# Layer 3's attention front moved under layer 2's third expert, and the targets' factor spread part by part

## The chip, the cores and the metric

One NeuronCore of a Trainium2 chip. The time is the device time of one execution in microseconds (us). Durations of single steps come from one profiled execution. In the profile the engines are PE (TensorE matmul), PEld (TensorE weight load), DVE (VectorE), ACT (ScalarE), POOL (GpSimd) and SP (SyncE, which issues DMAs); a "q" behind a name is that engine's sequencer. L12 is line 12 of the kernel before. Every fp32 matmul appears as two records in the trace, a transpose as one.

## The reference, cut to what matters

A graph of N = 2708 nodes with D = 256 features goes through four layers; each adds a graph step and a feed-forward step to x. What is touched here lies in layers 2 and 3:

```python
# layer 2, attention with one head
wh = h @ W
e = wh @ a[:F_OUT] + (wh @ a[F_OUT:]).T            # target part + source part
e = where(e > 0, e, 0.2 * e); e = where(adj > 0, e, NEG_BIG)
x = x + elu(softmax(e) @ wh)
# layer 2, four experts of 512 hidden units, two per node chosen by scores
for ei in range(4):
    hh = gelu(x @ W1[ei] + b1[ei]); out += g[ei] * (hh @ W2[ei] + b2[ei])
# layer 3, the same attention with four heads of 64 features (no elu), then a
# switch feed-forward of 8 experts with a capacity, one per token
```

Each of these steps reads a layernorm of x.

## The kernel before, in words

**Tiles.** Nodes lie in 22 tiles of 128 rows (the last has 20). Targets are taken in six chunks, five of 512 and one of 148 (CHUNKS). Layer 3's attention uses its own six parts: 256, four times 512, and 404. Loops are unrolled; the only branches in what follows are `tc.If`. Each engine works its instructions in one fixed order; a pool's buffers make an instruction wait until an earlier user of the same buffer is done.

**The attention** (`fast_gat`, L3402) needs no exponential per edge. With f the source part, r the target part and g the largest source part, a weight is adj × max(R[target], Q[source]) once V is scaled by B[source], where R = exp(.8(r + g)) with a bound, Q = exp(−.8(f − g)) and B = exp(f − g) (L3474–L3479). The order is:

1. *Front* (L3425–L3473): GpSimd clears fs and V's column of ones; the weights W and the vectors a are loaded, and VectorE puts W·a beside W (`pr`, L3439, L3445). `features` (L1610) norms x (statistics L1640, L1641, square root on ScalarE L1643, reciprocal L1644, result `fa` on ScalarE L1652 or VectorE L1654), transposes it on TensorE into `ft_ps`, and copies it to `fT` by a helper that alternates VectorE and ScalarE (`copy`, L99 and L101). Each node tile then takes two matmuls into `v_ps` (L3455), a ScalarE copy to V (L3462) and a VectorE copy to fs (L3465).
2. *Extremes* (L2826–L2842), the check of the range (L2849), rel, R, B and Q (to L3479); GpSimd scales V by B, tile by tile (L3482).
3. *Spread* (L141): R is a column per tile. For every chunk and head TensorE transposes it, broadcast over 128 columns, so that each partition holds R of all targets; the result is copied to Rr. All chunks and heads come ahead of the pass: 22 transposes a head, 88 with four heads.
4. *Pass*: for each part, source tile j and head, SyncE loads the adjacency block, VectorE makes the weight tile PT in one instruction (L3525) from Rr, Q and the block, and TensorE accumulates it against V (L3598 with one head, L3673 with four). There are 20 PT buffers (10 with one head). The 20 last source rows go in a short form (Rt, Qt, Vt). The part's end (`finish`, copies at L3557, transposes L3562) and the switch stage's logits and ranks (`after`) are generators of which one step is taken per source tile of the next part.

**Layer 2's experts** (`fast_l2_ffn`). `expert` (L4000) takes for one chunk four hidden blocks of two matmuls each into `h_ps` (2 PSUM buffers), a Gelu on ScalarE into hT (L4013), and then per node tile four matmuls into `y_ps` (L4019). Experts 0 and 1 are computed while the scores are formed, and parked; the parked values are added to x, weighted, by VectorE (L4067). Then expert 2 runs over the six chunks, its results added to x (L4056, L4057). Expert 3 stands behind in a branch on a flag that says whether any node uses it (L4072); with these inputs it is not taken, and the branch skips its body. After the branch comes the setup of the switch stage (`Switch`: constants on GpSimd, L4120 to L4156, weights by SyncE, copies on VectorE at L4262), and then layer 3's attention, in program order; a scheduler may move single instructions among those of other stages on the same engine.

Of the kernel before, what the change touches and what calls it, by code (L numbers as in the profile page):

```python
# [8 lines left out]
F32 = mybir.dt.float32  # L9
# [3 lines left out]
AF = mybir.ActivationFunctionType  # L13
# [5 lines left out]
N = 2708  # L19
D = 256  # L20
# [5 lines left out]
def sz(t):  # L26
    return 128 if t < NT - 1 else TAIL


def blocks(c0, cs):  # L30

    return [((c0 + o) // 128, o, min(128, cs - o)) for o in range(0, cs, 128)]
# [7 lines left out]
def brow(ap, n):  # L40

    return row(ap).to_broadcast([128, n])
# [3359 lines left out]
def fast_gat(k, adjT, W, a, H, elu, col, side, parts=CHUNKS, after=None):  # L3402
# [5 lines left out]

    nc, tc = k.nc, k.tc
    Fo = D // H
    with ExitStack() as ctx:
        keep = ctx.enter_context(tc.tile_pool(name="g", bufs=1))
        V = keep.tile([128, NT, H, Fo + 1], F32, name="V")
        Rr = keep.tile([128, H, N], F32, name="Rr")
        fs = keep.tile([128, 2, H, NT], F32, name="fs")
        R = keep.tile([128, H, NT], F32, name="R")
        Q = keep.tile([128, H, NT], F32, name="Q")
        B = keep.tile([128, H, NT], F32, name="B")  # L3420
        nc.gpsimd.memset(fs, 0.0)
        nc.gpsimd.memset(V[:, :, :, Fo : Fo + 1], 1.0)
        with tc.tile_pool(name="gf", bufs=1) as pf, tc.tile_pool(
            name="gt", bufs=2
        ) as tmp, tc.tile_pool(name="ps_g", bufs=3, space=PSUM) as psv:  # L3425
            fa = pf.tile([128, NT, D], F32, name="fa")
            fT = pf.tile([128, 2, N], F32, name="fT")

            w = pf.tile([128, 2, D + 2 * H], F32, name="w")
            nc.sync.dma_start(w[:, :, :D], W.rearrange("(k p) c -> p k c", p=128))  # L3430
            ar = pf.tile([128, 2, H, Fo], F32, name="ar")
            for s in range(2):
                nc.sync.dma_start(
                    ar[:, s, :, :].rearrange("p h f -> p (h f)"), brow(a[s], D)
                )
            for kk in range(2):
                for s in range(2):
                    pr = tmp.tile([128, H, Fo], F32, name="pr")
                    nc.vector.tensor_tensor(  # L3439
                        pr,  # L3440
                        w[:, kk, :D].rearrange("p (h f) -> p h f", h=H),
                        ar[:, s, :, :],
                        ALU.mult,
                    )
                    nc.vector.tensor_reduce(  # L3445
                        w[:, kk, D + s * H : D + (s + 1) * H], pr, AX.X, ALU.add
                    )
            def project(c0, cs):
                for t, _, p in blocks(c0, cs):
                    value(t, p)  # L3450

            def value(t, p):
                o = psv.tile([128, D + 2 * H], F32, name="v_ps")
                for kk in range(2):
                    nc.tensor.matmul(  # L3455
                        o[:p],
                        lhsT=fT[:, kk, t * 128 : t * 128 + p],
                        rhs=w[:, kk, :],
                        start=(kk == 0),
                        stop=(kk == 1),  # L3460
                    )
                nc.scalar.copy(  # L3462
                    V[:p, t, :, :Fo], o[:p, :D].rearrange("p (h f) -> p h f", h=H)
                )
                nc.vector.tensor_copy(  # L3465
                    fs[:p, :, :, t], o[:p, D:].rearrange("p (s h) -> p s h", s=2)
                )

            k.features(fa, fT, project)
            ex = extremes(k, fs[:, 1, :, :], H, pf, "gx")  # L3470
            spread_check(k, ex, H, col, pf)
            g = ex[:, 0, :, None].to_broadcast([128, H, NT])
            rel = pf.tile([128, H, NT], F32, name="rel")  # L3473
            nc.vector.tensor_tensor(rel, fs[:, 1, :, :], g, ALU.subtract)  # L3474
            nc.vector.tensor_tensor(R, fs[:, 0, :, :], g, ALU.add)
            nc.vector.tensor_scalar(R, R, 0.8, RANGE + 5.0, ALU.mult, ALU.min)
            nc.scalar.activation(R, R, AF.Exp)
            nc.scalar.activation(B, rel, AF.Exp)
            nc.scalar.activation(Q, rel, AF.Exp, scale=-0.8)  # L3479
            for t in range(NT):  # L3480
                p = sz(t)
                nc.gpsimd.tensor_tensor(  # L3482
                    V[:p, t, :, :],
                    V[:p, t, :, :],
                    B[:p, :, t, None].to_broadcast([p, H, Fo + 1]),
                    ALU.mult,
                )
            with tc.tile_pool(name="ps_gs", bufs=2, space=PSUM) as pss:
                for c0, cs in CHUNKS:
                    for h in range(H):  # L3490
                        k.spread(Rr[:, h, c0 : c0 + cs], R[:, h, :], c0, cs, pss)


        every = [h * (H == 4) for h in range(4)]
        last = slice(TAIL), NT - 1
        Vt = k.tail_rows(keep, "Vt", [Fo + 1], F32, [V[last[0], last[1], h, :] for h in every])
        Qt = k.tail_rows(keep, "Qt", [1], F32, [Q[last[0], h, last[1] :] for h in every])
        if H == 1:
            G = len(CHUNKS) - 1
            Rt = keep.tile([128, G + 1, 128], F32, name="Rt")  # L3500
            nc.gpsimd.memset(Rt[:, G, :], 0.0)
            for b in range(4):
                p = slice(32 * b, 32 * b + 32)
                nc.scalar.copy(
                    Rt[p, :G, :],
                    Rr[p, 0, : G * 512].rearrange("p (g b n) -> p b g n", b=4, n=128)[:, b],
                )
            for t, o, n in blocks(*CHUNKS[G]):
                p = slice(o // 4, o // 4 + 32)
                nc.scalar.copy(Rt[p, G, :n], Rr[p, 0, t * 128 : t * 128 + n])  # L3510
# [6 lines left out]
        if H > 1:  # L3517
            pst = ctx.enter_context(tc.tile_pool(name="ps_gt", bufs=2, space=PSUM))
# [3 lines left out]

        def product(PT, R, Q, aj):

            return nc.vector.scalar_tensor_tensor(PT, R, Q, aj, ALU.max, ALU.mult)  # L3525

        made = [None]

        def weights(c0, cs, j, h, aj):

            PT = ptp.tile([128, 512], F32, name="PT")
            made[0] = product(
                PT[:, :cs], Rr[:, h, c0 : c0 + cs], Q[:, h, j : j + 1], aj[:, :cs]
            )
            return PT
# [17 lines left out]
        def finish(c0, cs, i, acc, final):  # L3553
# [4 lines left out]
            yield  # L3558
            for t, o, n in blocks(c0, cs):
# [26 lines left out]

        for i, (c0, cs) in enumerate(parts):
            if H == 1:
# [3 lines left out]
                for j in range(NT - 1):  # L3592
                    PT = weights(c0, cs, j, 0, adjacency(c0, cs, j))
                    for (t, o, n), ac in zip(bl, acc):
                        if n == TAIL:
                            late.append((j, PT[:, o : o + n]))
                            continue
                        nc.tensor.matmul(  # L3598
                            ac[:n],
                            lhsT=PT[:, o : o + n],  # L3600
                            rhs=V[:, j, 0, :],
                            start=(j == 0),
                            stop=False,
                        )
                    if j % 4 == 3 or j == NT - 2:
                        for q, lhsT in late:
                            k.tail_targets(
                                acc[-1], q % 4, q < 4, q > NT - 6, lhsT=lhsT, rhs=V[:, q, 0, :]
                            )
                        late = []  # L3610
# [26 lines left out]
                if c0 + cs == N:  # L3637
                    for _ in side:
                        pass
# [322 lines left out]
def fast_l2_ffn(k, w, edges):  # L3962
# [7 lines left out]
    with ExitStack() as ctx:  # L3970
# [13 lines left out]
        ps1 = ctx.enter_context(tc.tile_pool(name="ps_m1", bufs=2, space=PSUM))  # L3984
# [15 lines left out]
        def expert(e, wt, c0, cs, use):  # L4000
            w1t, w2t = wt
            hT = hp.tile([128, M, 512], F32, name="hT")
            for m in range(M):
# [11 lines left out]
                )  # L4015
            for t, o, n in blocks(c0, cs):
# [9 lines left out]
                use(t, n, y)  # L4026

        with tc.tile_pool(name="el", bufs=1) as pl:
# [33 lines left out]

        for c0, cs in CHUNKS:
# [8 lines left out]
        with tc.If(nc.values_load(flag, min_val=0, max_val=1)):  # L4072
            for c0, cs in CHUNKS:
                expert(E - 1, wts[E - 1], c0, cs, add(E - 1))
# [417 lines left out]
def model(tc, I, out):  # L4492
# [4 lines left out]
    with tc.tile_pool(name="flags", bufs=1) as fp:  # L4497
# [4 lines left out]
        with ExitStack() as ctx:  # L4502
            k = Fast(ctx, tc, I["x"], bad, adjT)
            with tc.tile_pool(name="lists", bufs=1) as lp:
# [35 lines left out]
                fast_gat(k, adjT, I["L2_gnn_W"], I["L2_gnn_a"], 1, True, 2, iter(()))  # L4540
                fast_l2_ffn(k, part(I, "L2_ffn_"), edges)
# [4 lines left out]
            def after(c0, cs, i, psum):  # L4546
# [6 lines left out]
            fast_gat(  # L4553
                k, adjT, I["L3_gnn_W"], I["L3_gnn_a"], 4, False, 3, iter(()), parts, after
            )
# [60 lines left out]
```

## Time and profile before

| | |
|---|---|
| three runs | 2412.81, 2415.03, 2422.92 us; median 2415.03 us |
| the profiled execution | 2413.34 us, of which span 2411.6 us |
| TensorE | busy 2255.9 us, 94% of the span, mean granted clock 0.961 |
| VectorE | busy 1533.7 us, 64% |
| ScalarE | busy 666.4 us, 28% |
| GpSimd | busy 454.6 us, 19% |
| layer 2's expert 2 | TensorE from 1635.2 to 1710.2 us |
| layer 3's front and spread | to the first accumulation at 1776.1 us |
| part 0 of layer 3's pass | to 1808.2 us |
| parts 1 to 5 | to some 2140 us |

A line of the timeline gives the start, the busy time, the engine, the line and operation, output <- inputs, the shapes, how many records are put together (x10), and in brackets the idle time of the engine before it with what ended it. A line of the table of stretches gives start:end and its length, then for each engine the busy time in it (and how many instructions), then the mean granted TensorE clock (1.00 is full), the share of time in which the DMA engines moved data, and GB/s. VectorE also has to do with the part's end in the pass: its 63 us in a part of 512 are 88 weight tiles and some 16 small operations. Some whole-kernel rows:

```profile
L3673 PE MATMUL acc_ps<-PT,V 128*64 128x512 f32 (+4 forms) x2016 | 328.5, 549 | 0.4 <-ACT Rr L101 0.4
L3525 DVE SCALAR_TENSOR_TENSOR PT<-Rr,Q,aj 128x512 f32<-128x512 f32 (+3 forms) x630 | 408.4, 703 | 86.9 <-PE acc_ps L3598 75.1
L4006 PE MATMUL h_ps<-fT,w1t 128*128 128x512 f32 (+1 forms) x288 | 116.4, 554 | 0.3 <-ACT hT L4013 0.2
```

Columns: line, engine, operation, names and shapes, count; then busy us and mean ns of one; then the engine's idle time just before such an instruction, and what ended most of it.

### The profile page before, as it was taken

What the parts mean: (1) busy time and instruction counts of PE and PEld (TensorE: products, weight loads), DVE (VectorE), ACT (ScalarE), POOL (GpSimd) and SP (SyncE); (2) the same over time, 40 slices, a digit from 0 to 9 for tenths busy, and PEclk for the clock granted to TensorE, in tenths of its full rate; (3) what the DMA queues carried; (4) which work ended last, traced back from release to release, by engine and by line L of the source; (5) the groups of instructions that cost most, each with busy time, mean ns of one, the idle gap of its engine ahead of it and who ended that gap; (6) DMA issues with size and microseconds to landing.
All of it is one profiled execution on the core that took longest, in us unless ns stands there. A gap on an engine that the chain in (4) does not pass through costs nothing. (4 is left out here: it accounts for less than half of the span.)

```text
span 2411.6 us, 31812 instructions
## 1 busy us (share of the span) xinstructions
PE 2255.9 (94%) x11620; PEld 1500.7 (62%) x11620; DVE 1533.7 (64%) x3401; ACT 666.4 (28%) x1347; POOL 454.6 (19%) x496
## 2 busy tenths in 40 slices
PE   7999999989899899999799999999889999969997
PEld 4777765577778676777578876666642333325664
DVE  7588888645686558456565562342589999853544
ACT  5433343213655222212230013232321111111121
POOL 1100013004100233565130003420030000002221
PEclk9999999869999999999899998999899999979998
DMA  5244322200756243332245523000033443314430
GB/s 150 66 114 115 113 79 79 73 3 12 239 175 185 67 113 94 83 77 47 69 140 151 144 62 59 21 0 1 10 86 113 114 114 111 92 51 164 128 124 15
DMA packets 158572, 220.00 MB, mean 91 GB/s; under 512 B 30911, under 2 KB 94115, under 8 KB 158404
## 3 DMA queue, kind: packets, MB, share of 16 engines
q1 hardware_dynamic: 126096, 179.84, 25.5%
q0 software_dynamic: 15488, 24.04, 4.8%
q10 hardware_dynamic: 16820, 13.95, 1.8%
q8 instruction: 96, 1.57, 0.3%
q14 instruction: 72, 0.59, 0.1%
HBM read 193.49 MB, written 24.82 MB: 91 GB/s over the span
## 5 line engine op out<-in xcount | busy, mean ns | idle before, releaser
L3525 DVE SCALAR_TENSOR_TENSOR PT<-Rr,Q,aj 128x512 f32<-128x512 f32 (+3 forms) x630 | 408.4, 703 | 86.9 <-PE acc_ps L3598 75.1
L3673 PE MATMUL acc_ps<-PT,V 128*64 128x512 f32 (+4 forms) x2016 | 328.5, 549 | 0.4 <-ACT Rr L101 0.4
L3673 PEld LDWEIGHTS acc_ps<-PT,V 128*64 128x64 f32 (+1 forms) x2016 | 95.2, 122 | 210.2 <-issue 154.6
L1844 PE MATMUL acc_ps<-fa,PT 128*128 128x257 f32 x882 | 215.4, 383 | 1.2 <-DVE out L1864 1.2
L1844 PEld LDWEIGHTS acc_ps<-fa,PT 128*128 128x128 f32 x882 | 163.9, 190 | 66.5 <-issue 33.8
L3598 PE MATMUL acc_ps<-V,PT 128*128 128x257 f32 x882 | 195.4, 382 | 0.8 <-ACT Rr L101 0.6
L3598 PEld LDWEIGHTS acc_ps<-V,PT 128*128 128x128 f32 x882 | 165.8, 190 | 29.8 <-PE acc_ps L3598 2.3
L3304 PE MATMUL h_ps<-xT,w1t 128*128 128x384 f32 x512 | 176.5, 498 | 3.5 <-ACT xT L3295 3.5
L3321 PE MATMUL y_ps<-w2t,hT 128*128 128x256 f32 x768 | 169.8, 380 | 0.0
L2511 PE MATMUL acc_ps<-V,at 128*128 128x257 bf16 x1323 | 156.7, 277 | 10.1 <-DVE at L2502 8.2
L3321 PEld LDWEIGHTS y_ps<-w2t,hT 128*128 128x128 f32 x768 | 144.9, 190 | 21.1
L2511 PEld LDWEIGHTS <-at 128*128 128x128 bf16 x1323 | 128.9, 99 | 32.9 <-DVE at L2502 5.7
L3304 PEld LDWEIGHTS h_ps<-xT,w1t 128*128 128x128 f32 x512 | 95.9, 193 | 68.0 <-ACT xT L3295 8.5
L1816 ACT ACTIVATE PT<-s_ps,rq 128x512 f32<-128x512 f32 (+1 forms) x126 | 79.5, 637 | 174.3 <-PE s_ps L1792 168.7
L3333 POOL DMA_INDIRECT acc<-ys,ids x48 | 92.0, 1916 | 155.1 <-DVE ys L3330 144.7
L1792 PE MATMUL s_ps<-KT,QT 128*128 128x512 f32 (+1 forms) x252 | 116.2, 548 | 2.5 <-ACT PT L1816 1.6
L4019 PE MATMUL y_ps<-w2t,hT 128*128 128x256 f32 (+1 forms) x528 | 117.2, 379 | 0.0
L4006 PE MATMUL h_ps<-fT,w1t 128*128 128x512 f32 (+1 forms) x288 | 116.4, 554 | 0.3 <-ACT hT L4013 0.2
L3003 POOL DMA_INDIRECT xe<-fd,idg x48 | 79.7, 1661 | 194.7 <-DVE early_f L3034 180.3
L1817 DVE SCALAR_TENSOR_TENSOR PT<-aj,PT 128x512 f32<-128x512 int32 (+1 forms) x126 | 79.2, 633 | 57.9 <-ACT PT L1816 57.5
L4442 PE MATMUL y_ps<-w2t,hT 128*128 128x256 f32 (+1 forms) x512 | 112.8, 379 | 0.0
L4019 PEld LDWEIGHTS y_ps<-w2t,hT 128*128 128x128 f32 (+1 forms) x528 | 97.7, 186 | 22.3 <-issue 8.2
(743 smaller groups left out, 3353.0 us busy)
## 6 DMA issues: line engine op xcount, KB each, us to landing
aj<-in_adjT SPq DMA_DIRECT2D x399, 256.0 KB, 2.7
w1t<-in_L_ffn_W SPq DMA_DIRECT2D x8, 1024.0 KB
w2t<-in_L_ffn_W SPq DMA_DIRECT2D x8, 1024.0 KB
w1t<-in_L_ffn_w SPq DMA_DIRECT2D x8, 1024.0 KB, 5.6
w2t<-in_L_ffn_w SPq DMA_DIRECT2D x8, 1024.0 KB
aj<-in_adjT SPq DMA_DIRECT2D x63, 74.0 KB, 1.9
fd<-fa ACTq DMA_DIRECT2D x9, 512.0 KB, 3.2
aj<-in_adjT SPq DMA_DIRECT2D x21, 202.0 KB, 2.5
```

The lines of the kernel that those rows point to most:

```text
L1792: nc.tensor.matmul(s[:, :cs], lhsT=QT[:, j * 128 : j * 128 + 128], rhs=KT[:, c0 : c0 + cs], start=True, stop=True,)
L1844: nc.tensor.matmul(ac, lhsT=PT[:, o : o + n], rhs=fa[:, j, :], start=j == 0, stop=False)
L2511: nc.tensor.matmul(ac[:, c:], lhsT=at[:, o : o + n], rhs=V[:, j, r], start=j == 0 and q == 0, stop=False, skip_group_check=True,)
L3304: nc.tensor.matmul(hp, lhsT=w1t[:, kk, m * 128 : (m + 1) * 128], rhs=self.xT[:, kk, :], start=(kk == 0), stop=(kk == 1),)
L3321: nc.tensor.matmul(y, lhsT=self.hT[:, m, i * 128 : (i + 1) * 128], rhs=w2t[:, m, :], start=(m == 0), stop=(m == M - 1),)
L3333: add = nc.gpsimd.indirect_dma_start(out=acc, out_offset=bass.IndirectOffsetOnAxis(ap=self.ids[:, i : i + 1], axis=0), in_=ys, in_offset=None,
L3525: return nc.vector.scalar_tensor_tensor(PT, R, Q, aj, ALU.max, ALU.mult)
L3598: nc.tensor.matmul(ac[:n], lhsT=PT[:, o : o + n], rhs=V[:, j, 0, :], start=(j == 0), stop=False,)
L3673: nc.tensor.matmul(w.pop("out"), **w)
L4006: nc.tensor.matmul(o[:, :cs], lhsT=w1t[:, kk, m * 128 : (m + 1) * 128], rhs=fT[:, kk, c0 : c0 + cs], start=(kk == 0), stop=(kk == 1),)
L4019: nc.tensor.matmul(y[:n], lhsT=hT[:, m, o : o + n], rhs=w2t[:, m, :], start=(m == 0), stop=(m == M - 1),)
L4442: nc.tensor.matmul(y[:n], lhsT=hT[:, m, o : o + n], rhs=w2t[:, m, :], start=(m == 0), stop=(m == M - 1),)
```

## The change

**Front as an object.** The front and the factors become a class `GatFront`. `all` runs it at once as before (layer 2's attention, where the transposes and value products are asked for chunk by chunk as before; as scheduled, the transposes of all chunks are over sooner, ahead of more of the products). `chunk` is a generator that does one chunk of nodes in steps: norm, the two groups of transposes with their copy, and the value products tile by tile. `ready` forms the extremes and the factors, now R ahead of rel, and the check of the range after them; GpSimd's scaling of V ends it.

**Under the third expert.** In `fast_l2_ffn` the branch with expert 3 stands ahead of expert 2's chunks, and the loading of layer 3's W and a, the two memsets and the products with a (`then()`) are asked for just behind it. When expert 2 is through with a chunk, that chunk's front becomes `side[0]`, of which one step is taken after each hidden block and each node tile of the next chunk; what is left is done before the next. `h_ps` gets a third buffer, and a pool of three `v_ps` buffers stands beside it. Layer 3's tiles come from the other end of the on-chip memory, so that they wait for nothing of layer 2. As scheduled, the loads and the products then stand in the last stage of layer 1 on SyncE and VectorE, ahead of the reload of x, and the memsets of layer 2's front ahead of the last scatter on GpSimd. The setup of the switch stage comes behind `ready`.

**Spread by parts.** The pass begins after spread(0); spread(1) is taken in steps, one head a source tile, within part 0, and spread(i + 2) in part i + 1, between the two halves of part i's end. All its copies are on ScalarE, and it uses the `o_ps` buffers of the part's end. With one head the short form Rt of R is filled part by part too.

The diff, cut:

```diff
+class GatFront:
+    def __init__(self, k, W, a, H, pool, tmp):
...
+    def chunk(self, c0, cs, pool, psum):
+        k, bl = self.k, blocks(c0, cs)
+        t0 = bl[0][0]
+        fa = pool.tile([128, 4, D], F32, name="fa")
+        fT = pool.tile([128, 2, 512], F32, name="fT")
+        yield from k.norm_chunk(pool, fa, t0, len(bl))
+        for kk in range(2):
+            p = psum()
+            for t, o, m in bl:
+                k.nc.tensor.transpose(
+                    p[:, o : o + m],
+                    fa[:m, t - t0, kk * 128 : (kk + 1) * 128],
+                    k.ident[:m, :m],
+                )
+            k.copy(fT[:, kk, :cs], p[:, :cs])
+            yield
+        for t, o, m in bl:
+            self.value(t, m, lambda kk: fT[:, kk, o : o + m], psum)
+            yield
+
+    def ready(self, col):
...
+        ex = extremes(k, fs[:, 1, :, :], H, self.tmp, "gx")
+        g = ex[:, 0, :, None].to_broadcast([128, H, NT])
+        rel = self.tmp.tile([128, H, NT], F32, name="rel")
+        nc.vector.tensor_tensor(R, fs[:, 0, :, :], g, ALU.add)
+        nc.vector.tensor_scalar(R, R, 0.8, RANGE + 5.0, ALU.mult, ALU.min)
+        nc.scalar.activation(R, R, AF.Exp)
+        nc.vector.tensor_tensor(rel, fs[:, 1, :, :], g, ALU.subtract)
+        nc.scalar.activation(B, rel, AF.Exp)
+        nc.scalar.activation(Q, rel, AF.Exp, scale=-0.8)
+        spread_check(k, ex, H, col, self.tmp)
+        for t in range(NT):
+            p = sz(t)
+            vt = self.V[:p, t, :, :]
+            nc.gpsimd.tensor_tensor(
+                vt, vt, B[:p, :, t, None].to_broadcast([p, H, D // H + 1]), ALU.mult
+            )
...
-            with tc.tile_pool(name="ps_gs", bufs=2, space=PSUM) as pss:
-                for c0, cs in CHUNKS:
-                    for h in range(H):
-                        k.spread(Rr[:, h, c0 : c0 + cs], R[:, h, :], c0, cs, pss)
...
-        if H > 1:
-            pst = ctx.enter_context(tc.tile_pool(name="ps_gt", bufs=2, space=PSUM))
+        pst = ctx.enter_context(tc.tile_pool(name="ps_gt", bufs=2, space=PSUM))
...
+        def spread(i):
+            if i >= len(parts):
+                return
+            c0, cs = parts[i]
+            for h in range(H):
+                p = psum()
+                for t, o, n in blocks(c0, cs):
+                    nc.tensor.transpose(
+                        p[:, o : o + n],
+                        R[:n, h, t : t + 1].to_broadcast([n, 128]),
+                        k.ident[:n, :n],
+                    )
+                nc.scalar.copy(Rr[:, h, c0 : c0 + cs], p[:, :cs])
+                yield
+            if H == 1:
+                for t, o, n in blocks(c0, cs):
+                    p = slice(o // 4, o // 4 + 32)
+                    nc.scalar.copy(Rt[p, i, :n], Rr[p, 0, t * 128 : t * 128 + n])
+                yield
...
             for o_, ac in zip(oT, acc):
                 nc.scalar.copy(o_[:, :cs], ac[:, :cs])
             yield
+            yield from spread(i + 2)
...
+        for _ in spread(0):
+            pass
+        side = spread(1)
         for i, (c0, cs) in enumerate(parts):
...
                     PT = weights(c0, cs, j, 0, adjacency(c0, cs, j))
+                    next(side, None)
...
-                if c0 + cs == N:
-                    for _ in side:
-                        pass
+                side = spread(i + 2)
                 continue
...
-def fast_l2_ffn(k, w, edges):
+def fast_l2_ffn(k, w, edges, then):
...
-        ps1 = ctx.enter_context(tc.tile_pool(name="ps_m1", bufs=2, space=PSUM))
+        ps1 = ctx.enter_context(tc.tile_pool(name="ps_m1", bufs=3, space=PSUM))
...
                 nc.scalar.activation(
                     hT[:, m, :cs], o[:, :cs], AF.Gelu, bias=b1[:, e, m : m + 1]
                 )
+                next(side[0], None)
...
                 use(t, n, y)
+                next(side[0], None)
...
+        with tc.If(nc.values_load(flag, min_val=0, max_val=1)):
+            for c0, cs in CHUNKS:
+                expert(E - 1, wts[E - 1], c0, cs, add(E - 1))
+        steps = then()
         for c0, cs in CHUNKS:
...
             for e in range(EARLY, E - 1):
                 expert(e, wts[e], c0, cs, add(e))
-        with tc.If(nc.values_load(flag, min_val=0, max_val=1)):
-            for c0, cs in CHUNKS:
-                expert(E - 1, wts[E - 1], c0, cs, add(E - 1))
+            for _ in side[0]:
+                pass
+            side[0] = steps(c0, cs)
+        for _ in side[0]:
+            pass
...
+                right = dict(side="right")
+                keep = c3.enter_context(tc.tile_pool(name="g3", bufs=1, **right))
...
+                    two = c4.enter_context(tc.tile_pool(name="g3c", bufs=2, **right))
+                    ps = c4.enter_context(
+                        tc.tile_pool(name="ps_g3", bufs=3, space=PSUM, **right)
+                    )
...
+                    return lambda c0, cs: made[0].chunk(c0, cs, two, psum)
...
+            front = made[0]
+            front.ready(3)
+            c4.close()
```

## Prediction

> **What bounds the kernel now.** I read the mean clock and span first, then the table of stretches around the places that the diff touches, then the timeline inside the stretch in which TensorE idles, and last the chain of waits, to see that this stretch is on it. All times are us of one profiled execution.
>
> ```profile
> core 0: us, PE busy (x) PEld busy (x) DVE busy (x) ACT busy (x) POOL busy (x), PEclk, DMA share, GB/s
> ...
> 1709.00:1722.00 13.00, 1.40 (x7) 0.59 (x6) 9.07 (x39) 2.21 (x5) 3.20 (x17) 0.70 0.17 45
> 1722.00:1751.00 29.00, 28.82 (x132) 22.65 (x131) 16.27 (x74) 16.23 (x41) 0.00 (x0) 0.90 0.00 1
> 1751.00:1776.00 25.00, 16.57 (x91) 12.30 (x91) 20.36 (x45) 8.78 (x17) 18.71 (x30) 0.86 0.24 65
> 1776.00:1808.20 32.20, 32.12 (x354) 16.43 (x354) 29.94 (x72) 2.46 (x7) 0.00 (x0) 1.00 0.40 108
> 1808.20:1872.20 64.00, 64.00 (x372) 18.20 (x372) 63.61 (x103) 8.67 (x21) 1.71 (x2) 1.00 0.40 112
> 1872.20:1938.30 66.10, 66.10 (x390) 20.17 (x390) 62.80 (x105) 10.24 (x29) 4.20 (x4) 1.00 0.41 116
> ```
>
> The rows are: the end of layer 2's third expert to the first transpose of layer 3's front; that front (transposes, then the value products); the extremes and the spread of the factor R; part 0 of the pass (256 targets); parts 1 and 2 (512 each). TensorE is idle or cold only in the first three; in parts 1 and 2 both it and VectorE have almost no slack. The timeline says what each edge of the idle stretch waits for:
>
> ```profile
> 1721.84 2.37 PE L1610 MATMUL ft_ps<-ident,fa 128*128 128x128 f32 x10 [11.60 <-DVE fa L1654]
> ...
> 1754.37 14.66 POOL L3482 TENSOR_TENSOR V<-V,B 128x260 f32<-128x260 f32 x22 [38.58 <-ACT B L3478]
> ...
> 1766.38 1.58 DVE L3525 SCALAR_TENSOR_TENSOR PT<-Rr,Q,aj 128x256 f32<-128x256 f32 x2
> ...
> 1766.52 1.09 PE L141 MATMUL spread_ps<-ident,R 128*128 128x128 f32 x8 [1.02 <-DVE Rr L99]
> ...
> 1776.08 9.29 PE L3673 MATMUL acc_ps<-PT,V 128*64 128x256 f32 x100 [0.42 <-ACT Rr L101]
> 1778.62 26.75 DVE L3525 SCALAR_TENSOR_TENSOR PT<-Rr,Q,aj 128x256 f32<-128x256 f32 x66 [2.26 <-PE acc_ps L3673]
> ```
>
> TensorE stands 11.6 for the norm, and from 1754.74 to 1776.08 it does the spread alone, each eight transposes waiting for a copy that stands on VectorE behind two weight tiles PT. The first accumulation waits for the last copy. From the chain of waits:
>
> ```profile
> 1714.96 3.35 DMA w<-in_L_gnn_W
> ...
> 1768.62 3.72 PE spread_ps L141 x16
> 1772.36 0.59 ACT Rr L101
> ```
>
> **1. The branch, moved ahead of the third expert.** TensorE must now take it between expert 1 and expert 2. Its rows (L4072; min, median and max in ns, then first and last start):
>
> ```profile
> L4072 SPq COMPARE_BRANCH  x1: 50/50/50, 1578.1 to 1578.1; - x1
> ...
> L4072 PEldq COMPARE_BRANCH  x1: 3677/3677/3677, 1708.5 to 1708.5; - x1
> L4072 DVEq TENSOR_LOAD <-used x1: 544/544/544, 1711.3 to 1711.3; - x1
> L4072 DVEq COMPARE_BRANCH  x1: 72/72/72, 1711.9 to 1711.9; - x1
> ```
>
> Before, it is covered: it is over at 1712.2 and TensorE has no operand until 1721.8. Here the cover is gone. Its flag load waits for ScalarE's last Gelu of expert 1 (1632.17) and takes .49, so the branch runs from about 1633.5 to 1637.3, while queued y matmuls run on to 1635.2: **+2.1**. Bounds: 0 (prefetch reaches that far) and 5.2 (the load only after the last park). The Trainium skill, "Runtime: NRT & Kernel Launch", section "Instruction fetch mechanics", says that a taken branch whose target lies outside the two prefetched pages must fetch first; the row (3.68 on TensorE, .05 on SyncE) fits a long skipped body. What speaks against a gain is that the new place skips the same body with work waiting behind it; I take the row. Expert 2's matmuls stand behind that wait, and what follows on ScalarE and VectorE behind theirs, whose branches (.05 and .07 there) TensorE's covers.
>
> **2. Layer 3's front under expert 2.** The 44 transposes at .11 (4 in .44) and 88 product records at .2225 (16 in 3.56 warm) leave 1722–1751 and come as steps between expert blocks: 8 × .11 + 16 × .2225 = 4.4 a full chunk, at full clock, since the expert never idles TensorE (13.8 busy of 13.8 a chunk, clock 1.00). Beside it ScalarE gets per chunk two table loads (1.28 each), a square root .3, two fa at .55, one copy .6, four V copies at .37 and its four Gelus at .69: 9 of 18.7. VectorE has 3.6 of 13.8 busy now and gets some 5. I add 1.7 of stalls for the first chunk, since the 44 x-updates of experts 0 and 1 (L4067, .48 each, so 21) now queue behind the branch, and .5 for each later one: both estimates, of a few gaps like the .3 to .6 that the rows show between an engine and its releaser. End of expert 2's fourth chunk: 1637.3 + 13.8 + (18.2 + 1.7) + 3 × 18.7 = 1727.1. The tail is 6.2 expert and 4.4 front, then the last two tiles' front: norm, transposes, copy, products, about 4 by the rows at 1744–1751, plus 1.8 for VectorE waiting on GpSimd's setup of the next stage (queued ahead of the norm's reciprocal): 16.4. So the values end at **1743.5** against 1750.96. The W load and its products at 1715–1721, on the chain, go under earlier work: SyncE issues them some stages before, ahead of two small reloads, which costs those queues under .5 and no wait of TensorE. GpSimd's two memsets stand likewise ahead of one scatter; nothing is late by it.
>
> Here the skill speaks against the change: "ScalarE: Activation LUTs", section "What ACT_TABLE_LOAD costs", puts a set switch at 1.28 load plus 1.38 drain, 2.66. The rows show 1.28, and an ACTIVATE .02 after the load. By the row ten switches take 12.8, by the rule 26.6, of ScalarE, which has 9.7 a chunk to spare; so neither shows if the three h_ps banks (1.72 of matmul each) cover the Gelu's delay. I take the row.
>
> **3. R, spread(0), first PT.** From value end to R's exponential was 3.7; R now goes ahead of rel: 3.5. Then two transposes a head (.22, and .2 to the copy) and a ScalarE copy of 256 (.36): first PT 4.5 after the values, **1748.0** against 1758.02. No copy stands in VectorE's queue any more.
>
> **4. Part 0 then belongs to VectorE.** It needs 84 PT of 256. While GpSimd scales V (22 × .666 = 14.66, now from about 1747.6 to 1762.3) two PT take 1.58, .79 each, afterwards .405 (26.75 for 66). So 14.3/.79 = 18, then 66 × .405 = 26.7, to 1789.0; two tail tiles 1.3, and TensorE closes about 3 later (1808.2 against 1805.3 for the last of them now): **1793.3**. TensorE's own need (32.1, started at 1748.7) would end at 1781. Before: 1808.2. Gain 14.9. It holds 16 transposes of spread(1) for nothing, since TensorE waits there.
>
> **5. Parts 1 to 4** bear spread(2) to spread(5): 16 transposes × .11 = 1.76 each in a stage where TensorE is busy 64.0 of 64.0: **+7.0**. Copies are on ScalarE (10 of 66 busy): free. Bounds: 0 if these parts are really VectorE's (63.6 of 64.0 in part 1, then 62.8), 12 if each step breaks the flow for a wait on its bank.
>
> **6. Layer 2's attention.** There the same spread delays the first accumulation to 1237.17; with spread(0) alone and first R, 1234.3: −2.9. Six later transposes +.7, the front's new order (front over before the products of a chunk) +.7, between 0 and 1.6: **−1.5**.
>
> Sum, in which point 4 already holds 1 to 3: −14.9 + 7.0 − 1.5 = −9.4. The profiled run took 2413.34 (span 2411.6 and 1.7 around it), so 2403.9; the median of the runs shown is 1.7 above it, and I put the forecast on the median: 2415.0 − 9.4 = **2405.6**.
>
> **Rivals.** *More is kept* (chance .26): PT contention is the doubtful price. If the PT does not slow down, or parts 1 to 4 hide the transposes in waits, part 0 ends 18 × .385 = 7 earlier, or 5 to 7 of point 5 vanish: 2405.6 − 7 = 2398.6. For it: VectorE is just as full as TensorE in part 1, so some TensorE waits may lie inside what counts as busy. Against: .79 is measured six times over in a row. The skill's "SBUF — State Buffer", section "Who interferes with whom", calls the shared VectorE and GpSimd port an exclusive lock; .79 against .405 is a slowdown, not an exclusion, so I hold to the row: by a strict lock no PT would end before 1762 and part 0 would be about 7 later still.
>
> *Given back* (.17): the PT lead of 20 tiles that VectorE gathers during the present 21 us of spread is gone, so part 1 is paced by VectorE with every delay exposed; with 3 more in the tail and point 5 at 12 (5 more), 2405.6 + 8 = 2413.6. The change not doing what it says is this case too: if the steps' waits stretch the expert by what the front took alone.
>
> *Slower* (.05): one mechanism, table switches under expert 2. Sqrt and Gelu alternate in each chunk, and a square root waits for VectorE's statistics while the next Gelu stands behind it on ScalarE. From a delay of 3.4 (two h_ps banks ahead of TensorE) each further us is TensorE's. With the rule's 2.66 for all ten exposed: 26.6 − 9.4 = +17, 2432. Against: the norm's operands come from the chunk before.
>
> *The forecast* has .52, with its own range 2401 to 2410. What a measurement of this kernel can tell from no change is about .5%, 12.1: below 2403.0 counts as faster (nearly all of the first rival, and a quarter of the forecast: .39), above 2427.1 as slower (.04), the rest .57. The range 2395 to 2414 takes in both neighbours.
>
> **What would show it.** TensorE idles 2 before the third expert; a chunk there takes 18.2 to 19 at clock 1.00; values end 16 after chunk four; the first accumulation is at 1749 ± 2; part 0 ends on a wait for PT near 1793; parts 1 to 4 are 1.8 longer each. Wrong if expert 2 shows waits on hT, if PT during the scaling is not .79, or if parts 1 to 4 lengthen by over 3.

## The result and the profile after

The changed kernel takes 2408.75 us, median of 13 runs (2404.02 to 2413.79), against 2415.88 (2412.81 to 2424.33, 13 runs) for the kernel before: a ratio of 0.9966, 95% interval 0.9955 to 0.9977, so 8.2 us less (5.6 to 10.9). The forecast was 9.4 less. Its profiled run took 2408.92, span 2407.1. By size this is inside the forecast, but by luck: one of its terms was 6 too good and another 5.5 too bad.

The two spans differ by 4.5 only. The reason lies ahead of all that was changed in code for layer 3: in the front of layer 2's experts TensorE had a granted clock of 0.54 over 1455–1480 in the profile after, and 0.66 in that of before, and expert 0 starts at 1472.26 instead of 1469.45. The kernel of run e9 below, with the old code there, shows the same slow records (0.56 over the same stretch, expert 0 from 1472.77), so they come without the change too. To keep this out, I measure everything behind it from the end of expert 1 (1635.3 before, 1638.0 after). "Values" are the products of layer 3's front, and a part ends with its last accumulation:

| us after the end of expert 1 | before | forecast | after |
|---|---|---|---|
| expert 2 begins | 0 | 2.1 | 2.0 |
| values of layer 3 end | 115.7 | 108.2 | 106.2 |
| first accumulation | 140.8 | 113.4 | 111.9 |
| part 0 ends | 172.6 | 158.0 | 164.1 |
| parts 1, 2, 3, 4 take | 63.9, 66.1, 66.1, 66.0 | 1.8 more each | 62.3, 66.9, 67.0, 67.4 |
| end of the span | 776.3 | | 769.1 |

The table of stretches of the profile after, in the columns explained above: the wait for the branch; four chunks of expert 2, three of them with a front; the tail; extremes and spread(0); part 0; parts 1 and 2.

```profile
core 0: us, PE busy (x) PEld busy (x) DVE busy (x) ACT busy (x) POOL busy (x), PEclk, DMA share, GB/s
1638.00:1640.00 2.00, 0.06 (x2) 0.07 (x1) 0.00 (x0) 0.36 (x1) 0.71 (x1) 1.00 0.00 0
1640.00:1726.70 86.70, 86.70 (x337) 60.87 (x338) 43.64 (x134) 35.69 (x59) 0.00 (x0) 1.00 0.05 13
1726.70:1744.10 17.40, 13.89 (x69) 8.85 (x67) 8.47 (x33) 10.22 (x20) 2.94 (x15) 1.00 0.02 2
1744.10:1750.00 5.90, 2.92 (x13) 1.84 (x12) 3.35 (x15) 3.30 (x8) 2.50 (x4) 0.79 0.00 0
1750.00:1802.00 52.00, 51.32 (x385) 20.66 (x384) 51.28 (x102) 6.30 (x15) 17.82 (x27) 0.96 0.35 93
1802.00:1864.90 62.90, 62.90 (x378) 18.52 (x374) 56.51 (x92) 9.73 (x23) 1.64 (x2) 1.00 0.36 101
1864.90:1931.90 67.00, 67.00 (x407) 21.64 (x406) 63.17 (x106) 12.46 (x33) 3.82 (x4) 1.00 0.41 114
```

The 29 us in which TensorE did the front by itself are gone, and nothing was lost under expert 2: TensorE is busy 86.70 of 86.70. But part 0, 31.8 us from its first to its last accumulation before, takes 52.1. VectorE's timeline in the profile after, its weight tiles of part 0 and the short form of the last rows:

```profile
1748.89 41.84 DVE L3548 SCALAR_TENSOR_TENSOR PT<-Rr,Q,aj 128x256 f32<-128x256 f32 x86 [1.02 <-ACT Rr L3563]
1791.44 0.48 DVE L3548 SCALAR_TENSOR_TENSOR PT<-PT,Qt,aj 128x256 f32<-128x256 f32 x1 [0.72 <-ACT PT L3589]
```

VectorE is through with part 0 at 1791.9, as forecast; TensorE closes it at 1802.1, 10 later and not 3. By the rows of the timeline it is "busy" all that time. What it does is seen in the weight loads. Before:

```profile
1776.05 1.52 PEld L3673 LDWEIGHTS acc_ps<-PT,V 128*64 128x64 f32 x16 [0.49 <-issue]
1777.96 0.59 PEld L3673 LDWEIGHTS acc_ps<-PT,V 128*32 128x32 f32 x16 [0.39 <-issue]
1778.96 1.49 PEld L3673 LDWEIGHTS acc_ps<-PT,V 128*64 128x64 f32 x16 [0.41 <-issue]
```

After:

```profile
1784.56 0.14 PEld L3716 LDWEIGHTS acc_ps<-PT,V 128*32 128x32 f32 x2 [0.39 <-issue]
1785.11 0.20 PEld L3716 LDWEIGHTS acc_ps<-PT,V 128*64 128x64 f32 x4 [0.41 <-DVE PT L3548]
1785.69 0.15 PEld L3716 LDWEIGHTS acc_ps<-PT,V 128*32 128x32 f32 x6 [0.39 <-issue]
1786.25 0.19 PEld L3558 LDWEIGHTS o_ps<-ident,R 128*128 128x128 f32 x2 [0.41 <-issue]
1786.62 0.20 PEld L3716 LDWEIGHTS acc_ps<-PT,V 128*64 128x64 f32 x4 [0.17 <-issue]
```

Two source tiles come in two groups before: 16 records of 64-wide numerators from 1776.05, 16 of 32-wide denominators from 1777.96, the next at 1778.96: 2.9 for all. After, the scheduler has cut them into groups of two, four and six. A group takes .55 to .58 from one start to the next whether it holds two records or six, and between two groups the loads stand some .4. I call the passage from 64- to 32-wide accumulations, or back, a change of width. Counted in the instruction order of both programs, part 0 has 21 of them before and 50 after (51 by the starts in the trace); parts 1 to 5 have the same number in both, but for one more in part 1 of the trace.

What such a group costs can be worked out from the starts of all groups. In long groups the 64-wide records start in twos and the 32-wide ones in fours, one such step every .216 at 256 columns. A group takes its steps and .12 to .15 more: 16 numerator records 8 steps (1.88), 16 denominator records 4 steps (1.00). Two, four or eight denominator records take two steps all the same (.55 to .57). So a narrow group costs in two ways: one more change, and steps that are not filled.

### The profile page after: what moved, and what is told of

Its sections match the earlier page's. It is cut to its first block, busy times and chain, and to the rows that moved or that the text cites. A ratio compares the mean times of both kernels' runs of the same rounds, so it can differ in the third digit from the quotient of the medians.

```text
span 2407.1 us, 31811 instructions
## 1 busy us (share of the span) xinstructions
PE 2263.5 (94%) x11620; PEld 1501.1 (62%) x11620; DVE 1530.9 (64%) x3386; ACT 687.1 (29%) x1388; POOL 454.6 (19%) x496
## 5 line engine op out<-in xcount | busy, mean ns | idle before, releaser
L3716 PE MATMUL acc_ps<-PT,V 128*64 128x512 f32 (+4 forms) x2016 | 338.9, 551 | 0.7 <-DVE PT L3548 0.2
L1817 DVE SCALAR_TENSOR_TENSOR PT<-aj,PT 128x512 f32<-128x512 int32 (+1 forms) x126 | 79.2, 633 | 57.9 <-ACT PT L1816 57.5
```

The source lines that it names most:

```text
L3716: nc.tensor.matmul(w.pop("out"), **w)
```

## Experiments

All ratios are against the kernel before on the same chip, with 95% intervals. My theory after the result: **part 0 is held by TensorE's cut-up order**, and the spread by parts costs there most of what it brings. Rival: **VectorE's weight tiles hold it**, as forecast.

**e1, front alone.** The changed kernel with the spread as before:

```diff
+        with tc.tile_pool(name="ps_gs", bufs=2, space=PSUM) as pss:
+            for c0, cs in CHUNKS:
+                for h in range(H):
+                    k.spread(Rr[:, h, c0 : c0 + cs], R[:, h, :], c0, cs, pss)
...
-            yield from spread(i + 2)
...
-        for _ in spread(0):
-            pass
-        side = spread(1)
+        side = iter(())
```

> The changed kernel with the old spread: R of all parts is spread before the pass, copies on VectorE and ScalarE in turn; the front stays under expert 2. Theory (the spread by parts costs more than it brings, because TensorE's order in part 0 is cut into narrow groups): the values end as in the changed kernel, 9 to 10 earlier than before, measured from the end of expert 1, and everything behind is as before, part 0 taking 32 from its first accumulation; in all 9 to 10 us under the kernel before, about 2 under the changed one. Rival (the forecast's points 4 and 5: the spread by parts brings 15 - 7.5 and costs 7): within 1 us of the changed kernel or above it.

Measured: 0.9972 (0.9958 to 0.9985), 6.8 us less than before. Part 0 takes 31.8 from its first accumulation, with 21 changes of width, as before. So the front alone brings 6.8 of the 8.2, and the spread by parts on top of it not a difference that this can tell. The 9 to 10 expected were not reached; by its median this run is 1.0 above the changed kernel, which is what the rival had said, so the time doesn't speak for the theory. The profile, taken of the slowest of the 11 runs (2415.76), shows one reason: the values end 109.7 after expert 1 and not 106.2. The first hidden block of expert 2 and the last products ran at a lowered clock (0.70 over 1646–1650, 0.74 over 1745–1750), each just behind an idle stretch of 2.2 to 2.3. From the values to the end of part 0 it takes 57.6, the changed kernel 57.9.

**e2, spread alone.** The front stands behind the branch again (`front.all`), all else as in the changed kernel.

> The spread by parts alone: layer 3's front stands where it was before, behind the branch. Theory: the first accumulation comes about 19 earlier than before, but part 0 (54 changes between 64- and 32-wide matmuls instead of 21 in TensorE's order) takes some 52 instead of 32 us, and parts 1 to 4 about 1 more each: 1 to 4 us slower than before. Rival (part 0 is held by VectorE, as forecast): part 0 ends 7 earlier, the parts give 3 to 7 back: 0 to 4 us faster than before.

Measured: 1.0037 (1.0023 to 1.0051), 9 us slower than before, where the theory had 1 to 4. The first accumulation comes 21.8 earlier, and part 0 then takes 58.7. There is a second cause in it. The setup of the switch stage now stands on GpSimd behind the scaling of V, and a small VectorE instruction that needs it waits in the middle of the weight tiles:

```profile
1770.22 0.78 DVE L4207 TENSOR_SCALAR valid<-own 128x22 f32<-128x22 f32 x1 [4.97 <-POOL own L4174]
...
1771.06 9.24 PE L3716 MATMUL acc_ps<-PT,V 128*64 128x256 f32 x66 [5.11 <-DVE PT L3548]
```

Of the 27 by which part 0 is longer than before, 5 are that wait. The direction is the theory's; how much of the other 22 is the order's, this run does not tell.

**e3, order kept.** The accumulations of part 0 are chained on TensorE in the order of the code, with no semaphore between them:

```diff
+                    m = nc.tensor.matmul(w.pop("out"), **w)
+                    if i == 0 and line:
+                        tc.add_manual_dep(m.ins, line[-1].ins.name,
+                            mybir.DependencyInfo(
+                                mybir.DependencyClass.NoSync, mybir.DependencyReason.DATA),
+                            reason="in this order")
+                    line.append(m)
```

> The changed kernel with the accumulations of part 0 chained in the order of the code on TensorE (all 64-wide of two source tiles, then all 32-wide), 21 changes of width instead of 50. Theory (the order holds part 0): part 0 ends some 7 us earlier, about 3 after VectorE's last weight tile of it, and the time falls by 6 to 8 to about 2402. Rival (VectorE's weight tiles hold part 0): no change beyond 1 us. Second rival (parts 1 and 2, full on both engines, take it back): part 0 ends earlier and the time stays.

Measured: 0.9944 (0.9928 to 0.9961), 2402.13: 5.3 us below the changed kernel by the ratios, 6.6 by the medians; the intervals of the two still overlap by .0006, so the trace is what decides. VectorE's rows are those of the changed kernel, 3.1 later:

```profile
1751.99 41.85 DVE L3548 SCALAR_TENSOR_TENSOR PT<-Rr,Q,aj 128x256 f32<-128x256 f32 x86 [1.02 <-ACT Rr L3563]
1794.62 0.48 DVE L3548 SCALAR_TENSOR_TENSOR PT<-PT,Qt,aj 128x256 f32<-128x256 f32 x1 [0.78 <-ACT PT L3589]
```

TensorE's are others: part 0 takes 45.4 from its first accumulation instead of 52.1 and ends 3.4 after VectorE's last tile (1798.5 against 1795.1). The rival, that VectorE held part 0 already, falls. With the order kept, VectorE does hold it. A lowered clock doesn't explain the difference either: both profiles start part 0 at a granted clock of 0.50 for 4 us (1750–1754 in the changed kernel, 1753–1757 here).

**e4, no branch.** Expert 3 is left out, with its branch:

```diff
-        with tc.If(nc.values_load(flag, min_val=0, max_val=1)):
-            for c0, cs in CHUNKS:
-                expert(E - 1, wts[E - 1], c0, cs, add(E - 1))
         steps = then()
```

> The changed kernel with expert 3 and its branch left out (it is not taken with these inputs). Theory (TensorE waits 1.94 for the branch with nothing to cover it): expert 2 begins 1.9 to 2.2 earlier and the time is 2 us lower. Rival (that wait is slack that a later wait takes over, for instance VectorE's 44 updates of x under the first chunk): no change at the end of chunk 1.

Measured: 0.9961 (0.9946 to 0.9976). In the trace expert 2 follows without a gap, its first chunk ends 13.8 after expert 1 instead of 15.8, and the values 105.0 instead of 106.2. So the wait is no slack under the first chunk, as the rival had it; of the 2 that the branch costs at its place 1.2 is left at the values. The time is not told apart from the changed kernel's.

**e9, narrow groups in the kernel before.** To have the price by itself: two heads' numerators, then their denominators, chained, in part 0 of the kernel before.

```diff
+                if i == 0:
+                    todo = []
+                    for q in range(0, len(nums), 2):
+                        todo += nums[q : q + 2] + dens[q : q + 2]
```

> The kernel before, with part 0's accumulations put in narrow groups on purpose: two heads' 64-wide, then their 32-wide, 87 changes of width instead of 21, everything else as before. Theory (a change of width costs about .4 between the matmuls on its two sides): a group takes .55 to .58 whatever it holds, so part 0 takes 44 x 1.13 = 50 instead of 32 us, and the time rises by 15 to 18 us to about 2432. Rival (in the changed kernel TensorE was slow for waits on weight tiles that the profile counts as busy): no more than 2 us, since here VectorE has a lead of 20 tiles.

Measured: 1.0059 (1.0041 to 1.0077), 10 to 19 us slower; part 0 takes 50.1 where it took 31.8. Its weight loads, though VectorE starts with a lead of 20 tiles:

```profile
1791.02 0.14 PEld L3679 LDWEIGHTS acc_ps<-PT,V 128*32 128x32 f32 x4 [0.39 <-issue]
1791.57 0.20 PEld L3679 LDWEIGHTS acc_ps<-PT,V 128*64 128x64 f32 x4 [0.41 <-issue]
1792.16 0.14 PEld L3679 LDWEIGHTS acc_ps<-PT,V 128*32 128x32 f32 x4 [0.39 <-issue]
```

A pair of groups takes 1.14 (1791.02 to 1792.16), 44 of them 50. This is the same work in the same kernel; the order alone is shown to cost 18 us in part 0, for 66 more changes. That is .28 a change and not the .4 for which the loads stand. By the steps above, as an estimate, half of it is the changes (.12 to .15 each) and half that two heads' denominators take the two steps in which four heads' would go. The durations say so; no run keeps the two apart.

**e5, e6, e7: V scaled on ScalarE.** With GpSimd's scaling gone, the weight tiles should keep .41. e5 adds it to e3, e7 to the changed kernel alone, and e6 is e5 with the switch stage's setup asked for later.

```diff
+            if H == 4:
+                for h in range(H):
+                    nc.scalar.activation(
+                        vt[:, h, :], vt[:, h, :], AF.Copy, scale=B[:p, h, t : t + 1])
+                continue
```

> The changed kernel with part 0's accumulations chained in the code's order and layer 3's scaling of V by B moved from GpSimd to ScalarE (88 activations of 65 columns with a scale per row). With the order kept, part 0 is VectorE's: 84 weight tiles, of which those beside GpSimd's scaling took .63 on average over 31. Theory (what slows them is GpSimd's access): all at .41, the last tile of part 0 some 6 to 7 us earlier, part 0 ends 5 to 7 earlier than with the order alone, about 2396. Rival (TensorE with its 21 changes of width, 3.1 to 3.4 per pair of source tiles, holds part 0 by then): 2 us or less.

> As the run before it (order kept, V scaled on ScalarE), and the setup of the switch stage is asked for at the end of part 0 instead of ahead of the pass. Theory: the last two tiles' norm no longer stands behind VectorE's waits for GpSimd in the tail of expert 2 (TensorE idle 2.2 there), the values end 2 to 3 us earlier and so does everything behind: 2 to 3 us less. Rival (the setup then delays weight tiles of part 1): no gain.

> The changed kernel with the scaling of V on ScalarE alone, no chain. The program's order on TensorE then has 26 changes of width in part 0 by itself instead of 50. Theory (the number of changes holds part 0, the contention comes second): nearly the gain of both, 10 to 13 us under the changed kernel. Rival (only the contention counts, the order does not): the same as with order kept and V on ScalarE, but then the order alone would not have gained its 7.

Measured in the order e5, e6, e7: 1.0007 (0.9997 to 1.0016), 1.0014 (1.0007 to 1.0021) and 1.0012 (1.0003 to 1.0021): e5 15 us slower than e3, e7 11 slower than the changed kernel. All three missed for one reason, which I had not thought of. In e5's timeline:

```profile
1751.57 21.16 ACT L3513 ACTIVATE V<-V,B 128x65 f32<-128x65 f32 x88
...
1772.63 0.61 ACT L3569 COPY Rr<-o_ps 128x256 f32<-128x256 f32 x2
1773.00 0.88 DVE L3554 SCALAR_TENSOR_TENSOR PT<-Rr,Q,aj 128x256 f32<-128x256 f32 x2 [21.22 <-ACT Rr L3569]
```

The 88 scalings are ready at once, spread(0)'s copies only after their transposes; so the scalings stand first in ScalarE's queue and the first weight tile waits 21. What the runs do show is part 0 without GpSimd: 38.2 from the first accumulation in e5, and 84 tiles in 33.91; 39.3 in e7, which has 26 changes without any chain. In e6 the setup still stands on GpSimd ahead of the values' end (1741 to 1744), so it tells nothing of the tail; whether a later setup would help stays open.

**e10, the same with ScalarE's queue in order**: spread(0)'s copies, five tiles of V, a copy of spread(1), five tiles, and so on, chained as in e3.

> The changed kernel with part 0's accumulations in the code's order, and layer 3's V scaled on ScalarE, now held behind spread(0)'s copies there, with one copy of spread(1) after every five tiles. In the runs before, ScalarE took all 88 scalings (21 us) ahead of those copies, and the first weight tile came 21 late. Theory (GpSimd's access is what slows the first 31 weight tiles to .63): the first accumulation comes as in the changed kernel, part 0 takes 38 from there as in those runs (45 with the order alone, 52 in the changed kernel), and the time is 6 to 7 us below the run with the order alone, about 2395 to 2396. Rival (TensorE waits for the copies of spread(1) behind the scalings and gives it back): no gain over the order alone.

Measured: 0.9935 (0.9918 to 0.9952), 2397.66. The weight tiles have the theory's numbers:

```profile
1747.19 32.75 DVE L3549 SCALAR_TENSOR_TENSOR PT<-Rr,Q,aj 128x256 f32<-128x256 f32 x82 [0.27 <-ACT Rr L3581]
```

82 tiles at .40, against 86 in 41.85 with GpSimd beside them, the first 20 of those at .76. Part 0 takes 39.3 instead of 45.4, where the theory had 38. It ends 6.0 after the last tile now, so TensorE holds it again. The first accumulation comes 7.8 after the values and not 5.8 as in e3, which gives 2 of the 6 back: from the values to the end of part 0 it takes 47.1 against 51.2. The times of e3 and e10 (2 apart by the ratios, 4.5 by the medians) do not separate by their intervals; these 4 in the trace are what I rest on.

**e12, e13, e14.** All three are built on e10: the order kept in all parts (e12); then three (e13) or four (e14) source tiles to a group, with 24 weight buffers and 6 for the adjacency.

```diff
-            for j0 in range(0, NT, 2):
+            for j0 in range(0, NT, 3):
...
-                    if i == 0 and line:
+                    if line:
```

> As the run before it, with the order of the code kept in all parts. Only the last part changes: 21 changes of width there instead of 41. Theory (a change of width costs .43 between two groups of 404): 20 x .43 = 8.6 less, about 2387. Rival (in the last part TensorE waits for VectorE's ranks and copies anyway): 2 us or less.

> As the run before it, with three source tiles to a group instead of two (24 buffers for weight tiles instead of 20, 6 for the adjacency instead of 8): 14 to 16 changes of width a part instead of 21 or 22. Theory (about .54 a change at 512, .43 at 404, .4 at 256, as long as VectorE keeps up, which has 1 to 10% to spare in parts 1 to 4): up to 3 us less in each of parts 2 to 5, some 8 to 10 in all, about 2378. Rival (VectorE, full in these parts, holds them): 3 us or less.

> The same with four source tiles to a group and the same 24 buffers: 11 or 12 changes a part. The buffers hold one group of 16 weight tiles and half of the next, so VectorE must wait for the end of a group's last matmuls. Theory: what is saved in changes of width is lost in waits for weight tiles at the head of each group; within 4 us of the groups of three, on either side. Rival (only the number of changes counts): another 6 to 8 less.

Measured: 0.9910 (0.9896 to 0.9924), 0.9906 (0.9890 to 0.9923) and 0.9919 (0.9903 to 0.9935). In e12 the last part goes from 69.0 to 65.1: 3.9 of the 8.6 expected. Of the rest 2.4 is a longer wait for VectorE, .28 in e10:

```profile
2097.05 0.59 PE L4428 MATMUL misc_ps<-a_hv,a_hl 128*128 128x160 bf16 x6 [2.70 <-DVE a_hl L4421]
```

In e13 and e14 parts 2 to 4 take 67.8 to 68.3, not less than e12's 66.9 to 67.4, with 6 to 10 changes fewer each; the last part falls to 62.2 and 63.7. So the 8 to 10 expected of e13 did not come. That VectorE, 63 busy of 67, holds these parts is not what the traces show: in part 2 of e14 it waits 5.9 for weight tiles that TensorE has yet to free, and TensorE has no gap there. Rather, little was to be had. In part 2, 24 numerator and 24 denominator records take 8.01 in e13, and one and a half times e12's 16 and 16 take 8.16: by this some .15 for each change less, 1 us in a part. And it is spent again where transposes or other 128-wide matmuls fall inside a run of numerators, once in e12's part 2 and three times in e13's: two records cut off so take 1.00, and the 22 left as long as 24 would (5.29). By these durations e13 loses 2.0 by its two cuts more and wins 1.0; measured is .9 lost. e14 came within 4 of e13, as expected, but not by the waits at the head of each group that its theory had. What keeping the runs whole would bring was not tested. e12 and e13 beat both kernels, at 2394.04 and 2393.53, and their intervals lie below the changed kernel's.

## Why the forecast came out, point by point

The sum came out, but not as it was made up. In the table, the values come 9.5 earlier (forecast 7.5). From there to the end of part 0 it took 56.9 before and takes 57.9 now, where the forecast had 49.8: the spread by parts, meant to bring 7, brought nothing there. Parts 1 to 4 then give back 1.5 (forecast 7.0). That leaves 7.0, about the 7.2 at the end of the span, and all of it comes from the front under expert 2.

**1, the branch: right.** TensorE's wait is 1.94, forecast 2.1; the row is again long:

```profile
L4110 PEldq COMPARE_BRANCH  x1: 3404/3404/3404, 1636.2 to 1636.2; - x1
```

**2, front under expert 2: right, a little better.** A chunk with its front takes 18.2, the bare sum of 13.8 and 4.4; the 3.2 of stalls that I added did not occur. The tail took 17.4, forecast 16.4, with the wait for VectorE behind GpSimd's setup in it (2.22 before the last transposes). Table loads were 1.28 each with the next ACTIVATE .02 or less behind, without the drain that the Trainium skill ("ScalarE: Activation LUTs", "What ACT_TABLE_LOAD costs") adds, and TensorE waited for hT once, .34: the slower rival's mechanism is absent.

**3, first weight tile: right.** 4.7 after the values, forecast 4.5.

**4, part 0: the step that failed.** "TensorE's own need (32.1, started at 1748.7) would end at 1781", and "TensorE closes about 3 later". VectorE's side held: 20 tiles at .76 beside the scaling, then .40, and its end 153.9 after expert 1 (forecast 155). Where the Trainium skill ("SBUF — State Buffer", "Who interferes with whom") says how long its exclusive lock lasts, for VectorE's 2-port modes, it is a whole instruction and not a row of 22, so the prediction's "no PT would end before 1762" doesn't follow from it. Taking turns by whole instructions, a weight tile and a scaling would need .98, as an estimate from .40 and .58, their steps from start to start when alone. Both step at .76, so the measured row was the better choice.

On the other side I took TensorE's 32.1 from a stage that VectorE entered with 20 tiles made. When the tiles come one by one, the scheduler orders the accumulations by when it expects them, and 29 more changes of width, with the groups that they leave narrow, make TensorE the slower engine: it closed 10.1 behind VectorE, 7 more than forecast. e3 gives 6.7 of that back, e9 shows the price alone. The order of the instructions could have been counted before any run.

**5, parts 1 to 4: wrong in size, the other way.** Forecast +7.0, measured +1.5 for the four. Part 1 is 1.6 shorter: 12 of spread(2)'s 16 transposes were placed in part 0, and four of part 1's own accumulations stand ahead of part 0's last. The other three pay .8, .9 and 1.4 instead of 1.76. The transposes themselves are not cheaper than forecast: in part 2 groups of 3, 6, 7 and 8 take .48, .80, .91 and 1.02, .11 for each more. What came back lies elsewhere. In the kernel before, other matmuls cut two runs of numerators in each of parts 2 to 4, after the change one, and a run of 16 takes 3.58 whole, but 4.84 with one transpose behind its second record. By this estimate some 1.5 for the transposes less 1.0 for the cut is what was paid. So the two errors, +6 and −5.5, met by luck.

**6, layer 2: no gain.** From the first transpose to the end of its pass 243.9 both before and after; forecast −1.5. The first accumulation there now waits .93 for GpSimd's V instead of a copy of R.

## What to carry to other kernels

Where a change makes an operand come later or one at a time, look at the order in which the consumer's instructions are then emitted, not only at their sum: here long runs of one width were cheap, and each change cost .12 to .15, and a run of one or two heads' denominators as much time as one of four heads'. Work moved into another engine's queue had to be placed there by hand, since it was ready earlier than what the next stage waited for (e5, e10). And a term that is too good and one that is too bad can make a right total: compare stage by stage.

## What the runs showed of the hardware that I had not expected

- Narrow groups of 64- and 32-wide accumulations cost time by themselves: at 256 columns a group of four records takes .58 (64 wide) or .55 (32 wide), while 16 in a row take 1.9 or 1.0. Two denominator records take as long as eight.
- A VectorE weight tile and a GpSimd scaling, .40 and .58 from start to start alone, both step at .76 side by side.
- The same idle wait for the branch was followed by a granted clock of 1.00 in the changed kernel's profile and of 0.64 over 4 us in e3's, whose first hidden block took 8.80 instead of 7.10:

```profile
1639.85 8.80 PE L4061 MATMUL h_ps<-fT,w1t 128*128 128x512 f32 x16 [1.91 <-PEq L4121]
```

So a gap of 2 us may cost nearly 4. Single profiles differ by more than that: the values end 106.2 after expert 1 in the changed kernel and 109.3 in e3, and expert 1 itself ends at 1638.0 in the changed kernel, at 1633.9 in e12 and at 1641.9 in e4, which all have the same code up to there.
